# Attention with prompt tokens on one core: a context loaded earlier, its transposes three steps ahead, and first-stage work put in another order

## The chip, the cores and the metric

The kernel runs on one core of one Trainium2 chip. The metric is the device time in microseconds (us) of one execution. The engines are named as the profile names them: PE is TensorE's matmul stream (PEld its weight loads), DVE is VectorE, ACT is ScalarE, POOL is GpSimd, SP is SyncE. SP computes nothing here; it issues DMAs, in program order, and so does ACT's own queue (ACTq) in between ACT's instructions.

## The reference

Cross-attention over eight sequences. `x` is 8 x 112 x 320, the context 8 x 375 x 512, of which the last 4 tokens are image-prompt tokens and the first 371 are text. There are 20 heads of 16 channels. All is 32-bit floating point.

```python
q   = heads(x @ W_q)                               # 20 heads x 16
k_t = heads(text @ W_k);   v_t = heads(text @ W_v)
probs_t  = softmax(q @ k_t.T * 16 ** -0.5)
text_out = probs_t @ v_t
k_ip = heads(ip @ W_k_ip); v_ip = heads(ip @ W_v_ip)
qsem = l2norm(probs_t @ text)                      # per head
fused = q @ k_ip.T * 16 ** -0.5 + 0.5 * (qsem @ l2norm(ip).T)
ip_out = (softmax(fused) * mask) @ v_ip
out = (text_out + ip_out) @ W_out + b_out + x
```

## The kernel before

**Sequences and steps.** The eight sequences are numbered b = 0 to 7. The 20 heads are taken in five groups of four, so that there are 40 steps (b, g) with g = 0 to 4. The four heads of a group stand on the four 32-partition strips of TensorE.

**What a step does.** `multiplied` (L734) multiplies the transposed, unnormalised probabilities of the group, tile `xgT`, with the tile `u`, which holds the Gram matrix of the context, prompt columns and the group's values next to each other. Between its blocks TensorE computes the scores of the group two steps ahead (`scores`, L679), VectorE their negated maxima (`probabilities`, L692), ScalarE the exponentials (L696), and SP writes these probabilities into a ring of two tiles `xg` (L705). VectorE turns the next step's `xg` into `xgT` (`transposed`, L715), reduces the products in PSUM (`reduced`, L782), and GpSimd puts the next group's values into `u` (`placed`, L648). A function `between` then does a piece of the work for the next sequence on each step: the Gram matrix (L495), values (L571), keys (L537, or L528 for the last third of the heads), and queries (L332, L340).

**Where a sequence's data comes from.** `load_ctx` loads a context into a tile `ct`. Contexts 0 and 1 are loaded at the start and transposed on TensorE in three chunks (L410), each copied from PSUM into `ctxT` (L418 on VectorE, L420 on ScalarE). From context 2 on the load is laid out so that VectorE can do the transposing, in three instructions (L400), one in each of three steps. Such a load is eight DMAs on SP (L140, L145) and a small memset on GpSimd (L138). The Gram matrix is evacuated to the tile `ug` and from there written into `u` with four DMAs for each of four blocks (`gram_to_groups`, L513). Values go from `vext` to DRAM (`vd`, L587) and come back laid out for the groups (`vr`, four DMAs, L596).

**First stages.** Before step (0, 0) a fixed sequence of calls prepares sequence 0, and as much of sequence 1 as step (0, 0) needs: Gram matrix, values, queries (in six pieces), keys (in three), the scores and probabilities of steps (0, 0) and (0, 1), the transposes of context 1, and the first third of the values of sequence 1. On TensorE, SP and VectorE the order of the program is the order of execution everywhere; on ScalarE and GpSimd it is so in the first stages, and on ScalarE in the steps too. GpSimd's order in the steps is chosen by the scheduler.

**PSUM banks.** There are eight: four of a pool `ps_qd`, two of `ps_sc` for scores, and two of `ps_mm` for the rest. `bank(name)` takes one of `ps_mm`, or with `spare=True` one of `ps_sc`. In the first stages half of the early scores take banks of `ps_qd` as well. Context 1's transposes take banks of `ps_mm`.

**Where the loads of the steps stand.** `load_rest(n)` runs once in each step, after the reductions: step 0 loads two sequences of x, step 1 context 2 (`load_next(2)`), step 2 the output weights, step 3 the mask and the bias.

Of the kernel before, what the change touches and what calls it, by code (L numbers as in the profile page):

```python
# [20 lines left out]
def kernel(  # L21
# [63 lines left out]
    def bank(name, spare=False):  # L85

        if spare:
            return ps_sc.tile([P, 512], F32, tag="sc", name=name)
        return ps_mm.tile([P, 512], F32, tag="mm", name=name)
# [28 lines left out]
    def load_embed(eng, t, w):  # L118
        eng.dma_start(t[:, :, :C], w.rearrange("(p e) f -> p e f", e=NE))

    def spread(eng, t):

        v = t[:, :, FULL * P :].rearrange("p k (a r d) -> p k a r d", r=2, d=D)
        for a in (3, 2, 1):
            eng.tensor_copy(v[:, :, a, 0, :], v[:, :, a // 2, a % 2, :])
        eng.memset(v[:, :, :, 1, :], 0.0)
# [188 lines left out]
    def project_queries(bs):  # L315
        n = len(bs)
        xT = work.tile([P, NC, 2 * S], F32, tag="xT", name=f"xT_{bs[0]}", bufs=1)
        qm = work.tile([P, NC, 2, 2 * S], F32, tag="qm", name=f"qm_{bs[0]}", bufs=2)

        qT = const.tile([P, NC, S], F32, tag="qT", name="qT") if bs[0] == 0 else None  # L320
        for j, b in enumerate(bs):
            queries[b] = (qT, qm, j)
        nc.gpsimd.memset(xT[REST:, FULL, :], 0.0)
        for i in range(NC):
            cn = min(P, C - i * P)
            if bs[0] == 0:

                ps = ps_qd.tile([P, 512], F32, tag="qd", name=f"ps_x_0_{i}")
            else:
                ps = bank(f"ps_x_{bs[0]}_{i}", spare=bs[0] > 1 and i > 0)  # L330
            for j, b in enumerate(bs):
                nc.tensor.transpose(  # L332
                    ps[:cn, j * S : (j + 1) * S], x_sb[:, b, i * P : i * P + cn], ident[:S, :S]
                )
            nc.scalar.copy(xT[:cn, i, : n * S], ps[:cn, : n * S])
            yield
        for i in range(NC):
            ps = bank(f"ps_q_{bs[0]}_{i}")
            for j in range(NC):
                nc.tensor.matmul(  # L340
                    ps[:, : n * S],
                    wq_sb[:, j, i * P : (i + 1) * P],
                    xT[:, j, : n * S],
                    start=(j == 0),
                    stop=(j == NC - 1),
                )

            for r in range(2 if i < FULL else 1):
                nc.vector.tensor_scalar_mul(  # L349
                    qm[:, i, r, : n * S], ps[:, : n * S], emask[:, r : r + 1]  # L350
                )
            if qT is not None:
                nc.scalar.copy(qT[:, i, :], ps[:, :S])
            yield
# [37 lines left out]
    def transposed_context(b):  # L392
        begin(b)
        s = st[b]
        ct, ctxT = s["ct"], s["ctxT"]
        if b >= LEAD:

            for c in range(NT):
                some = slice(c * QN, (c + 1) * QN)
                nc.vector.transpose(  # L400
                    ctxT[:, :, c * P : (c + 1) * P].rearrange("p e (j i) -> p j e i", i=RG),
                    ct[:, some, :].rearrange("p j (k e) -> p j e k", e=NE),
                )
                yield
            return
        for c in range(NT):
            rows = min(P, TT - c * P)
            ps = bank(f"ps_c_{b}_{c}")
            for e in range(NE):
                nc.tensor.transpose(  # L410
                    ps[:, e * P : e * P + rows],
                    chunk(ct[:, c, :], e)[:rows],
                    ident[:rows, :rows],
                )
            o = ctxT[:, :, c * P : c * P + rows]
            i = ps.rearrange("p (e t) -> p e t", t=P)[:, :, :rows]
            if c % 2 and b < 1:
                nc.vector.tensor_copy(o, i)  # L418
            else:
                nc.scalar.copy(o, i)  # L420
            yield
# [84 lines left out]
            doubled(ps[c][:, : T - c * P], c, half[:, c])  # L506
            yield

    def gram_to_groups(b, blocks):

        for q in blocks:
            for a in range(GROUP):
                nc.sync.dma_start(  # L513
                    st[b]["u"][a * RG : (a + 1) * RG, q * GW : (q + 1) * GW],
                    ug[q * RG : (q + 1) * RG, :],
                )
# [69 lines left out]
    def values_to_dram(b, eng, c0=0, c1=NT):  # L586
        eng.dma_start(  # L587
            st[b]["vd"][c0 * P : c1 * P].rearrange("(c p) x -> p c x", p=P),
            st[b]["vext"][:, c0:c1, :C],
        )  # L590
# [460 lines left out]
    def drain(*gens):  # L1051
        for gen in gens:
            for _ in gen:
                pass
# [5 lines left out]
    def run(key, make, pieces=1):  # L1060

        if key not in gens:
            gens[key] = make()
        for _ in range(pieces):
            next(gens[key], None)

    def between(b, g):

        nb = b + 1
        new = nb < B  # L1070


        first = [bs for bs in pairs if bs[0] == (nb if b == 0 else nb + 1)]
        rest = [bs for bs in pairs if bs[0] == nb]
        if g == 0:
            if new:
                run(("g", nb), lambda: gram(nb), 2)
            if new:
                run(("g", nb), None)
            if b == 0:  # L1080
                run(("v", nb), None)
            if b > 0 and new:
                run(("f", b - 1), lambda: finish(b - 1))
        if g == 1:
            if new:
                run(("v", nb), lambda: values(nb), 1 if b == 0 else 2)
            if b == 0:
                run(("pp",), prompt_projections)
            for bs in first if b == 0 else ():
                run(("q", bs[0]), lambda: project_queries(bs), 3)  # L1090
        if g == 2 and new:
            run(("v", nb), None)
            run(("k", nb), lambda: keys(nb))
            for bs in first if b == 0 else ():
                run(("q", bs[0]), None)
        if g == 2 and b > 0 and new:
            run(("f", b - 1), None, 2)
        if g == 3:
            if new:
                run(("k", nb), None, 1)  # L1100
            if b > 0 and new:
                run(("f", b - 1), None)
            for bs in first if b > 0 else ():
                run(("q", bs[0]), lambda: project_queries(bs), 3)
            if b == 0:
                run(("t", b), lambda: prompt_logits(b))
            for bs in rest:
                run(("q", bs[0]), None)
        if 0 <= g - 2 * (b == 0) < NT and nb + 1 < B:
            run(("c", nb + 1), lambda: transposed_context(nb + 1))  # L1110
        if g == 4:
            if b > 0 and new:
                run(("f", b - 1), None, 2)
            if nb < B - 1:
                run(("k", nb), None, 1)
            for bs in (first if b > 0 else []) + rest:
                run(("q", bs[0]), None)
# [12 lines left out]
    order_values()  # L1130
    drain(products)
    nc.scalar.preload_act_table(AF.Exp)
    gram_to_groups(0, range(QN))
    run(("v", 0), lambda: values(0))
    run(("q", 0), lambda: project_queries(pairs[0]), 3)
    run(("v", 0), None, 2)
    values_to_dram(0, nc.scalar)
    spread(nc.gpsimd, wq_sb)
    nc.gpsimd.tensor_copy(wv_sb[:, :, C:], wk_sb[:, :, FULL * P : C])
    spread(nc.gpsimd, wk_sb)  # L1140
# [3 lines left out]
    for a in range(GROUP):  # L1144
        scores(0, 0, a, early=True)
        probabilities(0, 0, a)
    run(("q", 0), None)
    values_to_groups(0)
    for a in range(GROUP):
        if a == 2:  # L1150
            run(("k", 0), None)
        scores(0, 1, a, early=True)
        probabilities(0, 1, a)
    load_embed(nc.sync, wkip_sb, w_k_ip)
    load_embed(nc.sync, wvip_sb, w_v_ip)
    transposed(0, 0)
    placed(0, 0)
    drain(transposed_context(1))
    run(("k", 0), None)
    run(("v", 1), lambda: values(1))  # L1160
    more_constants()
# [5 lines left out]
    def load_rest(n):  # L1167

        if n == 0:
            load_x(1, 3)  # L1170
        elif n == 1:
            load_next(2)
        elif n == 2:
            load_channels(nc.sync, wo_sb, w_out)
        elif n == 3:
            nc.sync.dma_start(sm_sb, smask.unsqueeze(1))
            nc.sync.dma_start(bias_sb, b_out.partition_broadcast(S))
        elif n == NG:
            load_x(3, 5)
        elif n == 2 * NG:  # L1180
            load_x(5, B)
# [198 lines left out]
```

## Time and profile before

| | us |
|---|---|
| median of three timed runs | 436.21 |
| the three runs | 433.45, 436.21, 437.04 |
| the profiled execution, its own time | 437.43 |
| its span | 435.7 |
| mean granted clock of TensorE | 0.992 |
| first stages end, step (0, 0) begins | 40.36 |
| steps (0, 1) to (0, 4) begin | 52.76, 64.94, 74.30, 86.46 |
| step (1, 0) begins | 96.36 |

A step's beginning is the start of its first L734 on PE in the timeline. A line of the timeline has the start, the duration, the engine, the line of the kernel, the operation, what it writes and reads, the shape and the count; in brackets stands how long the engine was idle before it and what ended that idle time. Neighbouring instructions of one kind are merged into one line. SPq and ACTq are DMA issues on the queues of SP and ACT. A line of the list of waits has the waiting engine, tile and line, what it waited for, and the total in us, the number of waits and the longest one. A line of the table by stretches has the stretch, its length, and then for PE, PEld, DVE, ACT and POOL the busy time and the number of instructions, then the granted clock (1.00 is full speed), the busy share of the DMA engines and GB/s.

### The profile page before, as it was taken

To read this page: it belongs to the slowest core of one execution; us is meant where nothing else is said; L and a number is where in the kernel's file an instruction comes from. 1 tells how busy PE (TensorE), PEld (TensorE's weight loads), DVE (VectorE), ACT (ScalarE), POOL (GpSimd) and SP (SyncE) were. 2 spreads that over 40 slices of the span, in tenths; PEclk is the share of its full clock that TensorE was granted. 3 is DMA by queue.
4 is the path that set the end of the run, shared out by engine and by line. 5 is a ranking of instruction groups with operands and counts; after the bars stand their busy time and mean duration, and the time that the engine had idled before them with its cause. 6 is when DMAs were issued, how large, how long until landed. Compare 5 with 4: busy or idle time off the path is not lost. (4 is left out here: it accounts for less than half of the span.)

```text
span 435.7 us, 13984 instructions
## 1 busy us (share of the span) xinstructions
PE 420.6 (97%) x5521; PEld 328.1 (75%) x5521; DVE 325.9 (75%) x669; ACT 190.9 (44%) x663; POOL 111.9 (26%) x276
## 2 busy tenths in 40 slices
PE   8999999889999999999999999999999999999986
PEld 7856767668777887788777887788777887776783
DVE  5044468688797988888797988988787877878874
ACT  2352342223534363333535363433534353436793
POOL 6301100011133121602124111602124111526440
PEclk9998999989999999999999999999999999999999
DMA  7577357678556766458556766459565636553300
GB/s 253 150 186 214 90 129 170 162 174 192 130 156 144 180 171 164 128 141 205 138 147 147 171 139 168 123 134 205 133 168 133 160 89 179 150 146 106 95 4 26
DMA packets 57630, 64.26 MB, mean 147 GB/s; under 512 B 18448, under 2 KB 51592, under 8 KB 57566
## 3 DMA queue, kind: packets, MB, share of 16 engines
q1 hardware_dynamic: 57000, 62.66, 56.7%
q8 instruction: 43, 0.70, 0.7%
q10 hardware_dynamic: 566, 0.72, 0.5%
q14 instruction: 21, 0.17, 0.1%
HBM read 18.67 MB, written 5.32 MB: 55 GB/s over the span
## 5 line engine op out<-in xcount | busy, mean ns | idle before, releaser
L734 PE MATMUL ps_qd<-u,xgT 32*112 32x328 f32 (+11 forms) x3840 | 219.3, 353 | 0.6 <-POOL shared L769 0.6
L734 PEld LDWEIGHTS ps_qd<-u,xgT 32*112 32x112 f32 x3840 | 186.5, 172 | 34.4 <-issue 11.9
L715 DVE STREAM_TRANSPOSE xgT<-xg 128x1536 f32<-128x1536 f32 (+1 forms) x45 | 119.1, 2668 | 10.6 <-DMA xg<-p 9.8
L696 ACT ACTIVATE p<-ps_s,nmx 112x371 f32<-112x371 f32 x160 | 87.0, 581 | 85.9 <-DVE nmx L692 64.1
L692 DVE TENSOR_REDUCE nmx<-ps_s 112x1 f32<-112x371 f32 x160 | 77.6, 528 | 53.6 <-PE ps_s L679 52.4
L782 DVE CUSTOM_DVE_ANT_0 junk<-ps_qd,p 112x371 f32<-112x371 f32 x148 | 80.3, 543 | 15.5 <-ACT vext L578 0.5
L679 PE MATMUL ps_s<-kT,qm 32*112 32x375 f32 (+1 forms) x320 | 66.3, 484 | 0.7 <-ACT shared L765 0.7
L648 POOL COPY u<-vr 128x64 f32<-128x64 f32 x120 | 26.0, 237 | 154.1 <-PE ps_qd L734 104.8
L571 PE MATMUL ps_v<-wv_sb,ctxT 128*128 128x384 f32 (+1 forms) x192 | 63.6, 480 | 0.0
L571 PEld LDWEIGHTS ps_v<-wv_sb,ctxT 128*128 128x128 f32 x192 | 35.2, 190 | 19.7
L537 PE MATMUL ps_k<-ctxT,wk_sb 128*128 128x371 f32 x136 | 47.6, 494 | 0.0
L747 ACT COPY pvs<-ps_qd 112x21 f32<-112x21 f32 x150 | 15.7, 189 | 62.0 <-PE ps_qd L734 62.0
L537 PEld LDWEIGHTS ps_k<-ctxT,wk_sb 128*128 128x128 f32 x136 | 25.7, 196 | 15.5 <-issue 1.1
L679 PEld LDWEIGHTS ps_s<-kT,qm 32*112 32x112 f32 x320 | 26.8, 172 | 6.2 <-ACT kT L544 2.1
L495 PE MATMUL ps_g<-ctxT 128*32 128x375 f32 (+11 forms) x672 | 30.4, 333 | 0.0
L495 PEld LDWEIGHTS ps_g<-ctxT 128*32 128x32 f32 x672 | 27.7, 110 | 2.0
L698 ACT COPY ipl<-ps_s 112x4 f32<-112x4 f32 x140 | 23.5, 168 | 0.0
L578 ACT COPY vext<-ps_v 128x384 f32<-128x384 f32 (+1 forms) x24 | 11.2, 467 | 24.3 <-PE ps_v L571 24.3
L349 DVE TENSOR_SCALAR qm<-ps_q,emask 128x224 f32<-128x224 f32 (+1 forms) x25 | 9.1, 397 | 16.3 <-PE ps_q L340 16.2
L400 DVE STREAM_TRANSPOSE ctxT<-ct 128x512 f32<-128x512 f32 x18 | 19.9, 1104 | 0.0
L340 PE MATMUL ps_q<-xT,wq_sb 128*128 128x224 f32 (+1 forms) x90 | 17.8, 335 | 2.1 <-ACT kT L544 2.1
L544 ACT COPY kT<-ps_k 128x371 f32<-128x371 f32 x17 | 8.0, 470 | 24.7 <-PE ps_k L537 24.6
(167 smaller groups left out, 321.9 us busy)
## 6 DMA issues: line engine op xcount, KB each, us to landing
xg<-p SPq DMA_DIRECT2D x159, 162.3 KB
u<-ug SPq DMA_DIRECT2D x128, 99.0 KB
ct<-in_ctx_dram SPq DMA_DIRECT2D x24, 176.0 KB
vr<-vd SPq DMA_DIRECT2D x32, 120.0 KB
vip<-vipd SPq DMA_DIRECT2D x6, 560.0 KB
vd<-vext SPq DMA_DIRECT2D x7, 320.0 KB
vd<-vext SPq DMA_DIRECT2D x7, 160.0 KB
out_dram<-ob SPq DMA_DIRECT2D x8, 140.0 KB
```

The lines of the kernel that those rows point to most:

```text
L400: nc.vector.transpose(ctxT[:, :, c * P : (c + 1) * P].rearrange("p e (j i) -> p j e i", i=RG), ct[:, some, :].rearrange("p j (k e) -> p j ...
L495: nc.tensor.matmul(ps[c][q * RG : (q + 1) * RG, j * RG - c * P : T - c * P], ctxT[:, e, j * RG : (j + 1) * RG], ctxT[:, e, j * RG : T], st ...
L537: nc.tensor.matmul(ps[:, :TT], wk_sb[:, e, i * P : (i + 1) * P], s["ctxT"][:, e, :TT], start=(e == 0), stop=(e == NE - 1),)
L571: nc.tensor.matmul(ps[:, :w], ctxT[:, e, c * P : (c + 1) * P], wv_sb[:, e, :w], start=(e == 0), stop=(e == NE - 1),)
L648: nc.gpsimd.tensor_copy(v, dealt(b, c, s["vr"][:, c * QN : (c + 1) * QN, g, :]))
L679: nc.tensor.matmul(ps[:S, :w], qm[a * RG : (a + 1) * RG, i, r, j * S : (j + 1) * S], s["kT"][a * RG : (a + 1) * RG, i, :w], start=True, st ...
L692: nc.vector.tensor_reduce(nmx, ps[:S, :TT], AX.X, ALU.max, negate=True)
L696: nc.scalar.activation(p, ps[:S, :TT], AF.Exp, bias=nmx)
L698: nc.scalar.copy(s["ipl"][:, groups[g][a], :], ps[:S, TT:T])
L715: nc.vector.transpose(xT[:, j : j + n].rearrange("p j (k q) -> p q j k", q=QN), xg[:, :, j * RG : (j + n) * RG].rearrange("p q (j k) -> p ...
L734: nc.tensor.matmul(banks[a][:S, j * RG : UW], xT[a * RG : (a + 1) * RG, j, :S], region(b, c)[a * RG : (a + 1) * RG, q, j * RG - c * P :], ...
L782: nc.vector.tensor_tensor_reduce(out=junk, in0=ps[:S, :TT], in1=s["p", g][:, a, :], scale=1.0, scalar=0.0, op0=ALU.mult, op1=ALU.add, accu ...
```

## The change

Six things are edited, all in what is done for sequences 0, 1 and 2:

- Context 1's transposes run right after the first four scores, ahead of the last queries and the second keys. Their first two chunks take banks of `ps_qd`, the third one of `ps_mm`, and the third chunk is copied by VectorE (before, all three of context 1 were copied by ScalarE). For context 0 nothing changes in this.
- Context 2 is loaded at the end of the first stages instead of in step 1, and its three transposes run in steps 0, 1, 2 of sequence 0 instead of in steps 2, 3, 4.
- The second piece of the keys of sequence 0 runs ahead of all four scores of step (0, 1), not between the second and the third.
- The last of the four blocks of `gram_to_groups(0)` is issued on ScalarE's queue, after the first three pieces of the queries.
- `values_to_groups(0)` is issued on SP right after the write to `vd`, ahead of the writes of the first probabilities.
- The transposes of queries 1 and 2 take banks of `ps_sc` for their second and third part, as those of later queries did before. `placed(0, 0)` now stands ahead of `transposed(0, 0)`; they are on different engines.

```diff
@@ project_queries
-                ps = bank(f"ps_x_{bs[0]}_{i}", spare=bs[0] > 1 and i > 0)
+                ps = bank(f"ps_x_{bs[0]}_{i}", spare=i > 0)
@@ transposed_context
-            ps = bank(f"ps_c_{b}_{c}")
+            if b > 0 and c < 2:
+                ps = ps_qd.tile([P, 512], F32, tag="qd", name=f"ps_c_{b}_{c}")
+            else:
+                ps = bank(f"ps_c_{b}_{c}")
...
-            if c % 2 and b < 1:
+            if c == 1 + b:
                 nc.vector.tensor_copy(o, i)
             else:
                 nc.scalar.copy(o, i)
@@ gram_to_groups
-    def gram_to_groups(b, blocks):
+    def gram_to_groups(b, blocks, eng=nc.sync):
...
-                nc.sync.dma_start(
+                eng.dma_start(
@@ between
-        if 0 <= g - 2 * (b == 0) < NT and nb + 1 < B:
+        if g < NT and nb + 1 < B:
             run(("c", nb + 1), lambda: transposed_context(nb + 1))
@@ first stages
-    gram_to_groups(0, range(QN))
+    gram_to_groups(0, range(QN - 1))
     run(("v", 0), lambda: values(0))
     run(("q", 0), lambda: project_queries(pairs[0]), 3)
+    gram_to_groups(0, (QN - 1,), nc.scalar)
     run(("v", 0), None, 2)
     values_to_dram(0, nc.scalar)
+    values_to_groups(0)
...
     for a in range(GROUP):
         scores(0, 0, a, early=True)
         probabilities(0, 0, a)
+    drain(transposed_context(1))
     run(("q", 0), None)
-    values_to_groups(0)
+    run(("k", 0), None)
     for a in range(GROUP):
-        if a == 2:
-            run(("k", 0), None)
         scores(0, 1, a, early=True)
         probabilities(0, 1, a)
     load_embed(nc.sync, wkip_sb, w_k_ip)
     load_embed(nc.sync, wvip_sb, w_v_ip)
+    placed(0, 0)
     transposed(0, 0)
-    placed(0, 0)
-    drain(transposed_context(1))
+    load_next(2)
     run(("k", 0), None)
     run(("v", 1), lambda: values(1))
@@ load_rest
-        elif n == 1:
-            load_next(2)
```

## The prediction

> **What bounds the kernel now.** I read the page first, for the engine that is never short of work.
>
> ```profile
> span 435.7 us, 13984 instructions
> PE 420.6 (97%) x5521; PEld 328.1 (75%) x5521; DVE 325.9 (75%) x669; ACT 190.9 (44%) x663; POOL 111.9 (26%) x276
> ```
>
> TensorE is busy for 420.6 of 435.7 us. A change that leaves its matmuls alone, as this one does, can only save the rest: 15.1 us of idle time, and whatever is lost to a lower clock. So the second view was TensorE's own list of waits, from 28 to 110 us, where the edited lines run:
>
> ```profile
> PE ps_q L340 <- ACT kT L544: 2.1, 1, 2.1
> PE ps_k L528 <- ACT ipl L698: 1.9, 1, 1.9
> PE ps_c L410 <- ACT ctxT L420: 1.1, 1, 1.1
> PE ps_x L332 <- ACT ipkv L290: 0.7, 1, 0.7
> ```
>
> Four waits, 5.8 us, all beside edited lines. The third view was the table by stretches of half a microsecond, whose last columns are granted clock, DMA share and GB/s:
>
> ```profile
> 33.00:33.50 0.50, 0.50 (x3) 0.50 (x4) 0.28 (x1) 0.42 (x1) 0.00 (x0) 0.64 1.13 215
> ...
> 36.50:37.00 0.50, 0.50 (x3) 0.32 (x2) 0.00 (x0) 0.00 (x0) 0.44 (x2) 0.95 0.79 202
> ...
> 83.50:84.00 0.50, 0.00 (x0) 0.00 (x0) 0.50 (x3) 0.44 (x1) 0.00 (x0) 1.00 0.53 178
> ...
> 94.50:95.00 0.50, 0.50 (x3) 0.47 (x2) 0.36 (x3) 0.44 (x1) 0.05 (x1) 0.58 0.72 172
> ...
> 97.50:98.00 0.50, 0.50 (x8) 0.19 (x4) 0.02 (x1) 0.00 (x0) 0.16 (x2) 0.51 1.18 294
> ```
>
> The clock is granted at one half between these pairs of rows. A mean of 0.64 in the first means that the drop came at 33.14, a mean of 0.95 in the second that it ended at 36.55; the later stretch runs in the same way from 94.58 to 97.99. Each lasts 3.4 us at half speed, so each costs 1.7 us of matmul time. They follow the wait at 32 us and the one at 92 us; the wait at 83 us has no such tail.
>
> **The first stages.** The fourth view was the timeline. TensorE from the first scores to step 0 (start, duration):
>
> ```profile
> 24.70 0.89 PE L679 MATMUL ps_s<-kT,qm 32*112 32x371 f32 x8
> 25.52 0.92 PE L340 MATMUL ps_q<-xT,wq_sb 128*128 128x112 f32 x6
> ...
> 27.18 2.76 PE L537 MATMUL ps_k<-ctxT,wk_sb 128*128 128x371 f32 x8
> 30.68 1.23 PE L410 MATMUL ps_c<-ident,ct 128*128 128x128 f32 x8
> 32.99 1.04 PE L410 MATMUL ps_c<-ident,ct 115*128 115x115 f32 x4 [1.08 <-ACT ctxT L420]
> 33.22 2.94 DVE L715 STREAM_TRANSPOSE xgT<-xg 128x1536 f32<-128x1536 f32 x1 [1.37 <-DMA xg<-p]
> 33.83 4.02 PE L537 MATMUL ps_k<-ctxT,wk_sb 128*128 128x371 f32 x8
> 37.69 2.74 PE L571 MATMUL ps_v<-wv_sb,ctxT 128*128 128x384 f32 x8
> 40.36 1.22 PE L734 MATMUL ps_qd<-u,xgT 32*112 32x392 f32 x10
> ```
>
> The third transpose of context 1 waited 1.08 us for a bank, and the keys after it took 4.02 us where the same eight matmuls had taken 2.76. After the change the order is: scores of step 0, all twelve transposes, last queries, second keys, scores of step 1 together, third keys, values. At full clock these cost, from start to start, 0.82 (24.70 to 25.52), 1.85 (12/8 of 1.23), 0.85, 2.69, 0.82, 2.69 and 2.67 (37.69 to 40.36): 12.4 us. The 0.85 and 2.69 are 0.92 and 2.76 less 0.07, by which the 2.74 of the values runs into what follows. Step 0 could start at 37.1 instead of 40.36, 3.2 us sooner: 1.7 of it the clock, 1.1 the bank, 0.4 the scores of step 1, which now run in one block.
>
> VectorE now copies the third chunk out of its bank, and the second keys use that bank next. Such a copy was made once for context 0:
>
> ```profile
> 7.54 0.67 DVE L418 COPY ctxT<-ps_c 128x512 f32<-128x512 f32 x1
> ```
>
> It queues behind the maxima of step 0, about where the 0.85 us of queries run on TensorE. I take nothing, with its own 0.7 us as the upper bound; ScalarE is spared it.
>
> Now the queues that were reordered.
>
> ```profile
> 14.90 11.69 SPq L513 DMA_DIRECT2D u<-ug  x16
> 18.72 0.42 ACT L578 COPY vext<-ps_v 128x320 f32<-128x320 f32 x1 [1.59 <-PE ps_v L571]
> 20.68 0.82 PE L340 MATMUL ps_q<-xT,wq_sb 128*128 128x112 f32 x6
> 21.33 0.42 ACTq L587 DMA_DIRECT2D vd<-vext  x1
> 26.78 3.69 SPq L705 DMA_DIRECT2D xg<-p  x4
> 30.53 2.09 SPq L596 DMA_DIRECT2D vr<-vd  x4
> 43.19 1.74 SPq L705 DMA_DIRECT2D xg<-p  x2
> ```
>
> Four of the sixteen u writes go to ScalarE's queue. On SP one costs 0.73 us (11.69/16), on ScalarE the one issue shown costs 0.42. They fall into the 1.59 us that ScalarE idles before the copy at 18.72, and delay it by 0.1 to 1.3 us. That copy frees the bank of the queries at 20.68, so up to about 1.5 us is covered: cost nothing, at worst 0.5 if the issues slow one another down. SP is done with u at 23.7 instead of 26.6.
>
> The added wait is worse placed. The four vr reads now stand on SP ahead of the first xg writes, and they wait until vd, issued on ScalarE at 21.33, has landed. The DMA view of 24 to 25 us shows the last packets of ScalarE's queue:
>
> ```profile
> q10 hardware_dynamic: 10, 0.00, 1.3%
> ```
>
> So vd's data ends soon after 24, and with its completion lands at 24.5 to 26. Queued behind vr are the four xg writes of step 0, those of step 1, two prompt weights and the load of context 2. With vd landed at 25, vr is issued to 27.1 and the xg writes to 30.8, where they now end at 30.5. The transpose that starts at 33.22 then starts at 33.5 and ends at 36.5, in time for 37.1. At 26, or if vr's packets hold up xg's on the engines for their 2.09 us, it ends up to 2 us later and step 0 starts 1.5 us late. I take 0.3 us; below nothing it can't go, as TensorE is then the later one. First stages: 3.2 less 0.3 is 2.9 us.
>
> **The load of context 2, the eight DMAs.** They leave step 1 and go ahead of the write at 43.19, into a stretch in which SP has nothing else; there they cost nothing, since what is behind them (the xg of step 2) is transposed a whole step later. What they leave:
>
> ```profile
> 62.81 2.27 SPq L140 DMA_DIRECT2D ct<-in_ctx_dram  x4
> ...
> 66.48 4.19 SPq L513 DMA_DIRECT2D u<-ug  x4
> 67.11 1.03 ACT L696 ACTIVATE p<-ps_s,nmx 112x371 f32<-112x371 f32 x2 [1.72 <-DVE nmx L692]
> ...
> 73.33 2.48 SPq L513 DMA_DIRECT2D u<-ug  x4
> 75.92 1.83 SPq L705 DMA_DIRECT2D xg<-p  x2
> 80.25 2.95 DVE L715 STREAM_TRANSPOSE xgT<-xg 128x1536 f32<-128x1536 f32 x1 [3.15 <-DMA xg<-p]
> 85.13 1.40 PE L340 MATMUL ps_q<-xT,wq_sb 128*128 128x224 f32 x6 [2.13 <-ACT kT L544]
> ```
>
> The probabilities computed from 67.11 on can be written out only after 70.67, because SP is in the context load from 62.81 to 66.48 and then in u writes slowed by it (4.19 us against 2.48 for the next four). The other half goes out at 75.92, VectorE's transpose waits 3.15 us for it, the maxima and exponentials behind it slip, ScalarE's key copy with them, and TensorE stands for 2.13 us. Taking 3.7 us of issues and 1.7 us of slowing off SP puts every one of these writes over 3.15 us earlier, so VectorE doesn't wait. What is late next is the key copy itself, which follows its matmuls with the prompt logits in between: near nothing. Gain 2.1 us.
>
> **The three transposes of context 2** move from steps 2, 3, 4 to 0, 1, 2. Step 2 keeps one. In the other two they follow the reductions, where VectorE then idles:
>
> ```profile
> 54.35 0.99 DVE L692 TENSOR_REDUCE nmx<-ps_s 112x1 f32<-112x371 f32 x2 [5.13 <-PE ps_s L679]
> 66.53 0.99 DVE L692 TENSOR_REDUCE nmx<-ps_s 112x1 f32<-112x371 f32 x2 [4.96 <-PE ps_s L679]
> 87.30 1.09 DVE L400 STREAM_TRANSPOSE ctxT<-ct 128x512 f32<-128x512 f32 x1
> 93.89 0.54 PE L528 MATMUL ps_k<-ident,k 128*128 128x128 f32 x3 [1.88 <-ACT ipl L698]
> ```
>
> 1.09 us into gaps of 5.13 and 4.96 is free; without the cover, if context 2 landed more than 4 us into the gap, each would delay the maxima behind it. At 87.30 the transpose stands ahead of the maxima, the next big transpose and the maxima that the wait at 93.89 hangs on. Taking it out shortens that wait by 1.1 us, leaving 0.8. The half-speed stretch at 94.58 began after this wait; with 0.8 us of idling instead of 1.88 I take it as gone, 1.7 us. The transpose in step 4 stood beside reductions: nothing.
>
> **The query banks.** The 0.7 us wait of L332 goes, since two of its three banks now come from the scores' pair. But the next scores then wait for the copies out of these banks, so I take 0.3 of 0.7 (bounds 0 and 0.7).
>
> **The sum**, against the profiled execution's 437.43 us: 2.9 + 2.1 + 1.1 + 1.7 + 0.3 = 8.1, so 429.3 us. The three timed runs before spread from 433.45 to 437.04 around 436.21; two half-speed stretches are 3.4 us, so such stretches coming and going may be all of that spread, and the profiled run has both.
>
> **Rivals.** First, the half-speed stretches are not the waits' doing. For it: 2.13 us of idling at 83 us left the clock at 1.00. Against: both begin within 0.7 us of the end of a wait. Then 3.4 of the 8.1 us stay: 432.7 us. [...] The rows at 33 and 94 us speak against it, the row at 83 us for it. Chance 0.13.
>
> Second, SP stays late in steps 2 and 3 without the load, as the u writes alone keep it busy, so that the 2.13 us wait and what follows remain. Then only the first stages and 0.3 are won: 434.2 us. The 2.48 us of an undisturbed group speaks against it. Chance 0.09.
>
> Third, slower: the vr wait on SP. If vd lands late, xg, the transpose of step 0 and all later steps go with it, one for one from a landing at about 25.6 us. At 33.7 it has eaten the 8.1 us, and from 36.9 on the kernel is over 1% slower: 440.6 us. For it: vd now shares its queue. Against: its packets end soon after 24. Chance 0.08.
>
> **The numbers.** My forecast has 0.70: its own range is 427.5 to 431.5 (all of the 0.8 and 0.3 won too, or 1.5 us lost to vr and 0.5 to ScalarE's queue). To hold the first rival and half of the second the range goes from 427.0 to 433.5. A change of 1%, about what a measurement of this kernel can tell, is 431.85 against the median. Faster by over 1%: 0.70 and the lucky end of the first rival, 0.71. Within 1%: 0.21, the first two rivals. Slower: 0.08.
>
> **What would show it.** In the changed kernel: step 0's first L734 at 37 to 38 us; no wait of L410 on L420; eight context DMAs on SP before step 0; the clock at 1.00 from 30 to 40 and from 80 to 100; L715 in step 3 with no wait for xg; L340 with no 2 us wait in step 3; L528's first wait below 1 us. The forecast is wrong if vr's wait on SP moves step 0 beyond 40 us, if context 2 isn't there when VectorE comes to it in step 0, or if half-speed stretches appear elsewhere.

## The result and the profile after

The changed kernel's median is 432.05 us (15 runs, 430.63 to 435.12), against 435.32 us before (15 runs, 433.45 to 438.43): the ratio is 0.9913, with a 95% interval of 0.9886 to 0.9939. That is 3.3 us by the medians, a gain, but below the 1% line. The forecast of 429.3 us was 2.8 us too low. The time lies outside the forecast's own range, 427.5 to 431.5, and inside the one that was widened to hold two rivals, 427.0 to 433.5. Of its chances, 0.71 stood on a gain over 1% and 0.21 on less; it was less.

The profiled execution took 432.11 us, with a span of 430.1 us, 5.6 us less than the span of the profile before; TensorE's idle time in it fell from 15.1 to 11.3 us. The page, and TensorE's list of waits over the whole span (the tile and line that waited, for what, us in total, times, longest):

```profile
span 430.1 us, 13979 instructions
...
PE 418.8 (97%) x5521; PEld 327.3 (76%) x5521; DVE 326.8 (76%) x670; ACT 190.1 (44%) x662; POOL 111.6 (26%) x276
```

```profile
PE ps_w L430 <- POOL ident masks.py:199: 1.5, 1, 1.5
PE ps_qd L737 <- DVE xgT L718: 1.3, 1, 1.3
PE ps_k L531 <- ACT ipl L701: 1.1, 1, 1.1
PE ps_a L891 <- ACT bT L972: 1.0, 1, 1.0
...
PE ps_k L540 <- DVE ctxT L421: 0.2, 1, 0.2
```

Three of the four waits shown before are gone. The key transposes in step 4 (now L531) still wait, 1.1 us. L430 waits at the very start, as it did before; L737 and L891 lie in the last 20 us. Lines of the kernel after the edit to the context transposes are three higher than before.

The timeline of the first stages in the changed kernel:

```profile
25.00 0.89 PE L682 MATMUL ps_s<-kT,qm 32*112 32x371 f32 x8
...
25.17 1.88 SPq L599 DMA_DIRECT2D vr<-vd  x4
...
25.82 1.70 PE L413 MATMUL ps_c<-ident,ct 128*128 128x128 f32 x12
...
27.14 9.53 SPq L708 DMA_DIRECT2D xg<-p  x8
...
28.40 2.76 PE L540 MATMUL ps_k<-ctxT,wk_sb 128*128 128x371 f32 x8 [0.21 <-DVE ctxT L421]
...
33.81 2.97 DVE L718 STREAM_TRANSPOSE xgT<-xg 128x1536 f32<-128x1536 f32 x1
...
37.19 1.22 PE L737 MATMUL ps_qd<-u,xgT 32*112 32x392 f32 x10
```

Twelve transposes run in one piece of 1.70 us, the second keys wait 0.21 us for VectorE's copy, the transposition of the probabilities starts without waiting for the DMA, and step 0 begins at 37.19 us: 12.19 us after the first scores, where the sum had 12.39. SP's vr issue at 25.17 shows vd's landing, which the sum had at 25.

Later in the changed kernel:

```profile
73.35 2.95 DVE L718 STREAM_TRANSPOSE xgT<-xg 128x1536 f32<-128x1536 f32 x1
...
79.38 1.40 PE L340 MATMUL ps_q<-xT,wq_sb 128*128 128x224 f32 x6
...
82.30 0.99 DVE L695 TENSOR_REDUCE nmx<-ps_s 112x1 f32<-112x371 f32 x2 [0.67 <-PE ps_s L682]
...
87.22 0.54 PE L531 MATMUL ps_k<-ident,k 128*128 128x128 f32 x3 [1.08 <-ACT ipl L701]
...
89.57 0.17 PEld L737 LDWEIGHTS ps_qd<-u,xgT 32*112 32x112 f32 x1 [0.43 <-DVE ss L785]
```

The first two rows carry no bracket: in step 3 neither VectorE nor TensorE waits any more. The last row is new. At the start of step (1, 0) TensorE waits for VectorE's reductions of step (0, 4) (L785), which free the PSUM banks.

The starts of the steps, from the first L734 (L737) of each on TensorE, for the profiled execution of every kernel of this study but the last (e10), whose edit lies behind them. The labels are those of the experiments; the column of (0, 4) and (1, 0) is their sum.

| us | step 0 begins | (0,1) + (0,2) | (0,3) | (0,4) + (1,0) | (1,1) begins |
|---|---|---|---|---|---|
| before, first profile | 40.36 | 21.54 | 12.16 | 20.32 | 106.78 |
| before, second profile (e5) | 39.12 | 21.53 | 11.96 | 18.70 | 103.72 |
| changed | 37.19 | 21.04 | 10.08 | 18.48 | 99.19 |
| e1, before with fillers | 38.81 | 21.53 | 12.46 | 19.37 | 104.57 |
| e2, first stages only | 36.85 | 21.03 | 11.60 | 18.69 | 100.58 |
| e3, load only | 38.80 | 21.53 | 10.09 | 18.50 | 101.33 |
| e4, load early, turned late | 37.29 | 21.04 | 10.08 | 18.68 | 99.49 |
| e6, query bank back | 37.38 | 21.54 | 10.09 | 18.47 | 99.88 |
| e7, SP order back | 36.90 | 21.04 | 10.10 | 18.46 | 98.90 |
| e8, two sums off VectorE | 37.16 | 21.04 | 10.09 | 17.76 | 98.45 |
| e9, e8 with fillers near the end | 37.38 | 21.04 | 10.08 | 17.77 | 98.68 |

The first scores start anywhere from 24.66 to 25.20 us, so the first column has 0.5 us of its own scatter. From there to step 0 it is 12.18 or 12.19 us in every kernel with the new first stages, and 14.10 or 14.11 in e1, e3 and e5. Step 0 itself takes 12.40 or 12.41 us in all of them.

### The profile page after: what moved, and what is told of

Same layout as the page of the kernel before. It is cut to its first block, busy times and chain, and to the rows that moved or that the text cites. A ratio compares the mean times of both kernels' runs of the same rounds, so it can differ in the third digit from the quotient of the medians.

```text
span 430.1 us, 13979 instructions
## 1 busy us (share of the span) xinstructions
PE 418.8 (97%) x5521; PEld 327.3 (76%) x5521; DVE 326.8 (76%) x670; ACT 190.1 (44%) x662; POOL 111.6 (26%) x276
## 5 line engine op out<-in xcount | busy, mean ns | idle before, releaser
L737 PE MATMUL ps_qd<-u,xgT 32*112 32x328 f32 (+11 forms) x3840 | 220.1, 353 | 1.3 <-DVE xgT L718 1.3
L737 PEld LDWEIGHTS ps_qd<-u,xgT 32*112 32x112 f32 x3840 | 187.0, 172 | 34.5 <-issue 10.9
L718 DVE STREAM_TRANSPOSE xgT<-xg 128x1536 f32<-128x1536 f32 (+1 forms) x45 | 119.1, 2667 | 11.4 <-DMA xg<-p 10.8
L785 DVE CUSTOM_DVE_ANT_0 junk<-ps_qd,p 112x371 f32<-112x371 f32 x148 | 80.2, 542 | 15.5 <-ACT kT L536 0.5
L540 PE MATMUL ps_k<-ctxT,wk_sb 128*128 128x371 f32 x136 | 46.3, 483 | 0.2 <-DVE ctxT L421 0.2
L400 DVE STREAM_TRANSPOSE ctxT<-ct 128x512 f32<-128x512 f32 x18 | 20.0, 1109 | 1.9 <-DMA ct<-in_ctx_dram 1.9
L581 ACT COPY vext<-ps_v 128x384 f32<-128x384 f32 (+1 forms) x24 | 11.3, 471 | 21.2 <-PE ps_v L574 21.2
L471 POOL TENSOR_TENSOR ug<-ug,half 128x128 f32<-128x128 f32 (+1 forms) x24 | 10.4, 446 | 32.0 <-ACT ug L470 32.0
L928 POOL TENSOR_TENSOR wv<-vip,w 112x1280 f32<-112x1280 f32 x6 | 14.8, 2465 | 14.2 <-DVE w L868 14.2
```

The lines of the kernel that those rows point to most:

```text
L400: nc.vector.transpose(ctxT[:, :, c * P : (c + 1) * P].rearrange("p e (j i) -> p j e i", i=RG), ct[:, some, :].rearrange("p j (k e) -> p j ...
L540: nc.tensor.matmul(ps[:, :TT], wk_sb[:, e, i * P : (i + 1) * P], s["ctxT"][:, e, :TT], start=(e == 0), stop=(e == NE - 1),)
L718: nc.vector.transpose(xT[:, j : j + n].rearrange("p j (k q) -> p q j k", q=QN), xg[:, :, j * RG : (j + n) * RG].rearrange("p q (j k) -> p ...
L737: nc.tensor.matmul(banks[a][:S, j * RG : UW], xT[a * RG : (a + 1) * RG, j, :S], region(b, c)[a * RG : (a + 1) * RG, q, j * RG - c * P :], ...
L785: nc.vector.tensor_tensor_reduce(out=junk, in0=ps[:S, :TT], in1=s["p", g][:, a, :], scale=1.0, scalar=0.0, op0=ALU.mult, op1=ALU.add, accu ...
```

## The experiments

**e1: the clock.** The kernel before, with matmuls of no use in two of its waits.

```diff
@@ transposed_context, ahead of the third chunk of context 1
+            if (b, c) == (1, NT - 1):
+                fill = ps_qd.tile([P, 512], F32, tag="qd", name="ps_fill_0")
+                for _ in range(4):
+                    nc.tensor.matmul(fill[:, :P], ident, ident, start=True, stop=True)
@@ keys, ahead of the last third of sequence 1
+            if (b, i) == (1, FULL):
+                fill = bank("ps_fill_1")
+                for _ in range(7):
+                    nc.tensor.matmul(fill[:, :P], ident, ident, start=True, stop=True)
```

> The kernel before, with matmuls of no use put into two of its waits: four of 128 columns ahead of the third transpose of context 1 (wait of 1.08 us) and seven ahead of the key transposes in step 4 (wait of 1.88 us). They write banks that nobody reads. Theory 'the waits bring the half-speed stretches': with the waits filled the clock stays at 1.00 from 30 to 40 us and from 90 to 100 us, the third keys take 2.8 us instead of 4.0, and the mean clock of the runs is 0.999 or so; the median falls by what such stretches cost in the typical run of before, 0.5 to 2 us (434.8 to 433.3). [...]

The median was 434.62 us against 434.86 (ratio 0.9983, 0.9956 to 1.0011): no difference. Three of its 12 runs had a mean clock below 0.998, against 10 of the 35 runs of before beside it, so the fillers did not make half speed clearly rarer, and 12 runs are few to tell; none of the 12 went as low as 0.992, as 5 of the 35 did. In the profile the clock stayed up at 32 and 92 us, and step 0 began at 38.81, but a half-speed stretch came after the wait that had been left unfilled, at 83 us, where the first profile of before had none. The theory did not come out as written: in the profiles the stretches follow waits, but not the same waits in each execution.

**e2: the first stages alone.** The changed kernel without the load and the turning of context 2.

```diff
-        if g < NT and nb + 1 < B:
+        if 0 <= g - 2 * (b == 0) < NT and nb + 1 < B:
...
-    load_next(2)
...
+        elif n == 1:
+            load_next(2)
```

> The changed kernel with the load of context 2 put back into step 1 and its three transposes into steps 2, 3, 4: only the first stages and the query banks are changed. Theory 'the parts add, each at its place': step 0 begins at 37.2 as in the changed kernel, step 1 takes 11.2, but steps 3 and 4 take 12.2 and 9.5 to 9.9 again; step (1, 1) begins 3.5 to 4 us earlier than before's 106.78, and the median is 1.5 to 2.5 us under before (433.0 to 433.8). Rival 'what is won early is taken back later, whatever it was': the end is as early as in the whole change, 432, with steps of sequences 1 to 6 shorter than the changed kernel's.

Median 433.26 us, ratio 0.9964 (0.9934 to 0.9993), within the forecast of the additive theory. Step 0 begins as in the changed kernel; step 3 keeps its wait (11.60 us). Not as expected: steps (0, 4) and (1, 0) take 18.69 us, almost what they take in the changed kernel, though the transposes of context 2 stand in step 4 again. Step (1, 1) begins 6.2 us earlier than in the first profile of before, more than any theory had, but 3.1 us earlier than in the second (e5).

**e3: the load alone.** The kernel before with the opposite edits: `load_next(2)` behind `placed(0, 0)`, and the transposes in steps 0, 1, 2.

> The kernel before with only this changed: context 2 is loaded at the end of the first stages and turned in steps 0, 1, 2. Theory 'the parts add': step 0 begins at 40.4 as before, steps 3 and 4 take 10.1 and 8.1 to 8.5 instead of 12.2 and 9.9, no half speed after 92 us; step (1, 1) begins 3.5 to 4.5 us earlier than before's 106.78; the median is 1.5 to 2.5 us under before. Rival 'taken back later': 432 as for the whole change. If SP's long stop at the last DMA of the load costs something here, steps 0 and 1 are longer than 12.4 and 12.2.

Median 432.85 us, ratio 0.9945 (0.9925 to 0.9965). Step 3 falls to 10.09 us, and step (1, 1) begins 2.4 us earlier than in e5. By the ratios e2 wins 0.36% and e3 0.55%, together 0.91%, against 0.87% for the whole: within the intervals the parts add. The rival that either part ends as early as the whole falls for e3: at a mean clock of 0.998 or more its median is 432.65 us (11 runs), against 431.08 of the changed kernel (13 runs). For e2 it isn't excluded, with 431.88 in six such runs. Against the 434.69 of before beside them (25 runs) these are gains of 2.0 and 2.8 us, more together than the 3.6 of the whole, so part of the gain may be taken back later. In this execution step 0 began at 38.80 us with the wait of 1.1 us for the transpose bank in place: no half speed followed it.

**e4: load early, turn late.** The changed kernel with the old condition in `between` alone.

> The changed kernel with the load early, but the three transposes of context 2 back in steps 2, 3, 4. Theory 'it was the SP queue in step 3 and VectorE in step 4': step 3 takes 10.1 to 10.3, as in the changed kernel, since SP is free; step 4 and its wait for the prompt logits of the next scores grow by about 1.1 us (L531 waits 1.9 to 2.2 instead of 1.1); the median is 0.5 to 1.5 us over the changed kernel. Rival 'VectorE's transposes caused the wait in step 3 as well': step 3 takes 11 us or more.

Step 3 took 10.08 us, so SP's queue was its cause, as the theory said. But step 4's wait (L531) was 1.2 us, not 1.9 to 2.2, and the pair of steps 18.68 against 18.48. At a mean clock of 0.998 or more the median is 431.09 us (6 runs), the changed kernel's 431.08 (13 runs). At that clock, moving the three transposes is worth nothing that can be measured; the load is what counts. The median over all runs, 432.82 us (0.9930, 0.9902 to 0.9958), lies within the theory's 0.5 to 1.5 us over the changed kernel, but because 6 of its 12 runs had a mean clock below 0.998, against 2 of 15 of the changed kernel. Whether the later transposes bring half speed more often was not settled.

**e5: before, once more.**

> The kernel before, unchanged, for one more profiled execution. Theory 'the half-speed stretches come and go, and the sum of the prediction took two of them for granted': 25 of 35 timed runs of before had a mean clock of 0.998 or more, so most likely this one has none or one; without any, step 0 begins at 38.8 (not 40.4), the wait at 92 us costs about 1.2, steps (0, 4) and (1, 0) together take 18.6 (not 20.3), and step (1, 1) begins at 103.5 to 104.5 (not 106.8). Rival 'the stretches belong to the waits': both are there again and the table is that of the first profile.

This execution took 439.4 us with a mean clock of 0.992, and both stretches lay elsewhere. TensorE's waits from 20 to 110 us:

```profile
PE ps_q L340 <- ACT kT L544: 1.9, 1, 1.9
PE ps_k L528 <- ACT ipl L698: 1.2, 1, 1.2
PE ps_c L410 <- ACT ctxT L420: 1.1, 1, 1.1
PE ps_x L332 <- ACT ipkv L290: 0.7, 1, 0.7
...
```

The table by stretches of the same execution (the column before the last two is the clock):

```profile
422.50:423.00 0.50, 0.00 (x0) 0.00 (x0) 0.50 (x2) 0.50 (x7) 0.00 (x0) 1.00 0.00 0
...
423.50:424.00 0.50, 0.50 (x6) 0.50 (x6) 0.39 (x3) 0.50 (x1) 0.00 (x0) 0.84 0.00 0
...
430.50:431.00 0.50, 0.50 (x6) 0.50 (x5) 0.00 (x0) 0.00 (x0) 0.00 (x0) 0.83 0.00 0
```

All four waits of the prediction are there, and the clock stayed at 1.00 behind each. Instead it fell at 423.8 and came back at 430.7, twice 3.4 us; a wait of 1.0 us near the end had ended 0.7 us before the fall, and one of 1.3 us 8.3 us before it. The wait at 92 us was 1.88 in the first profile and is 1.2 here. The theory's times hold: the pair of steps takes 18.70 us, and step (1, 1) begins at 103.72. This is the undisturbed account of before up to step (1, 1): 103.72 us, of which the change wins 4.5, not 7.6.

**e6: the query bank.** The changed kernel with `spare=bs[0] > 1 and i > 0` again.

> The changed kernel with the transposes of queries 1 and 2 back in banks of ps_mm. Forecast of the term 0.3 us, the step table said 0.5 (steps 1 and 2 together 21.54 before, 21.04 after): steps 1 and 2 take 12.2 and 9.35 again, 21.5 together, and step 3 begins 0.5 us later. Rival 'the bank only moves the wait to the scores': 21.0 to 21.1 together.

Steps 1 and 2 took 21.54 us together, as before, and 21.04 with the edit: 0.5 us, the theory's figure.

**e7: the order on SP and ScalarE's queue.**

```diff
-    gram_to_groups(0, range(QN - 1))
+    gram_to_groups(0, range(QN))
...
-    gram_to_groups(0, (QN - 1,), nc.scalar)
...
-    values_to_groups(0)
...
     run(("q", 0), None)
+    values_to_groups(0)
     run(("k", 0), None)
```

> The changed kernel with the queue order of before in the first stages: all sixteen u writes on SP, and the vr reads after the first four writes of probabilities. Theory 'the order of these DMAs neither cost nor won': step 0 begins at 37.2 to 37.6, and the median is that of the changed kernel within 0.5 us. Rival 'vr was what held step 0, so moving it ahead was needed': GpSimd puts the values of step 0 in place at 36 to 38.5 and step 0 begins at 38 us or later, 0.8 us or more lost.

Step 0 began at 36.90 us, earlier than either theory had, but its first scores were earlier too: 12.19 us lie between them, as in the changed kernel. The median was 431.63 us (0.9928, 0.9893 to 0.9963). The timeline shows how near it was:

```profile
35.69 0.59 POOL L651 COPY u<-vr 128x64 f32<-128x64 f32 x3 [7.35 <-DMA vr<-vd]
...
36.90 0.60 PEld L737 LDWEIGHTS ps_qd<-u,xgT 32*112 32x112 f32 x10 [0.55 <-POOL k L215]
```

With vr behind the probabilities the values are in place at 36.3 us, 0.6 us before TensorE wants them. The two edits to these queues neither cost nor won anything that shows.

**e8: VectorE in step 4.** The changed kernel with the helper `shared` for two of the four reductions of step (0, 4).

```diff
-        if n == len(steps) - NG - 1:
+        if n == len(steps) - NG - 1 or n == NG - 1:
             sums = shared(b, g, GROUP // 2)
             next(sums)
             reduced(b, g, 2)
...
+        if n == NG - 1:
+            next(sums)
+        if n == NG:
+            drain(sums)
```

> The changed kernel with two of the four reductions of step (0, 4) taken from VectorE: ScalarE copies the two products out of PSUM, GpSimd multiplies, ScalarE sums. Theory 'steps (0, 4) and (1, 0) are held by VectorE's row of maxima, turn, maxima and four reductions, which frees the PSUM banks of the next step': (1, 0) falls from 10.35 to 9.9 or less, the pair from 18.5 to 18.0. Rival 'the pair is held by TensorE and the wait for the scores of (1, 1)': the pair stays at 18.4 or more. The median moves by less than can be told, 0.5 us at most.

Step (1, 0) fell from 10.35 to 9.63 us, the pair from 18.48 to 17.76:

```profile
87.54 0.87 ACT L768 COPY shared<-ps_qd 112x371 f32<-112x371 f32 x2
...
88.82 1.22 PE L737 MATMUL ps_qd<-u,xgT 32*112 32x392 f32 x10
```

These are rows of its timeline. ScalarE has emptied two banks by 88.4 us, and the ten matmuls at 88.82 run through. The bound of the pair was VectorE's row of work. The median, 431.52 us of 5 runs (0.9918, 0.9889 to 0.9947), can't show so little.

**e9: the same with fillers near the end.**

```diff
@@ multiplied, ahead of the first block
+        if (b, g) == (B - 1, NG - 1):
+            for _ in range(5):
+                nc.tensor.matmul(banks[0][:, :P], ident, ident, start=True, stop=True)
@@ finish
-                warm(ps, 3)
+                warm(ps, 6)
```

> The kernel of the run with two sums off VectorE, with matmuls of no use in two waits of the last steps: five in the bank of the last step's first product, ahead of it, and three more ahead of the last but one sequence's output sums (six instead of three). They overwrite nothing that is kept. In two of the profiled executions a half-speed stretch began just after these waits of 1.0 to 1.3 us. Theory 'short waits near the end bring half speed in some executions': of its runs at most 1 in 10 has a mean clock below 0.998 (13 of 49 runs of before, 11 of 43 of the kernels with the whole change or nearly so), and the median is 430.6 to 431.3, under the changed kernel's 432.05. Rival 'the fillers change nothing': a quarter of the runs below 0.998 as before, median 431.3 to 432.

Median 430.91 us of 6 runs (429.51 to 431.74), ratio 0.9889 (0.9850 to 0.9929), and none of the 6 below 0.998, while 5 of the 11 runs of before beside it were: as the theory had it. It is the fastest kernel of the study by its median. That it beats the changed kernel is not shown: the intervals overlap, and of e8's 5 runs, without the fillers, none had half speed either.

**e10: one long wait.**

```diff
+        if n == 3 * NG + 3:
+            late = const.tile([P, P], F32, tag="late", name="late")
+            nc.sync.dma_start(late, ehs[0, :P, :P])
+            fill = bank("ps_late")
+            nc.tensor.matmul(fill[:, :P], late, ident, start=True, stop=True)
```

> The changed kernel with one long wait of TensorE in step (3, 3): a matmul of no use that reads a tile whose load SP issues only in that step, behind the step's probabilities; 3 to 6 us of waiting. Theory 'half speed comes by chance after a wait, the likelier the longer it is': the mean clock lies below 0.998 in nearly all of its runs, with a stretch of 3.4 us or more behind this wait, and the time is the changed kernel's plus the wait plus 1.7 us, 436 to 440 in all. Rival 'the stretches have nothing to do with waits': about a quarter of the runs have one, and the time is 435 to 438.

All four runs had a mean clock of 0.990 to 0.992. The median was 439.46 us (1.0103, 1.0047 to 1.0160), 7.4 us over the changed kernel. Clock and time are those that the theory named, and the rival falls ("the likelier the longer" stands on this one length, 6.0 us, beside the waits of 0.9 to 1.9 us of other executions). The list of waits has the new one, and the table by stretches the clock behind it:

```profile
PE ps_late L1222 <- DMA late<-in_ctx_dram: 6.0, 1, 6.0
```

```profile
228.00:229.00 1.00, 0.00 (x0) 0.00 (x0) 0.00 (x0) 0.00 (x0) 0.00 (x0) 0.50 0.64 168
...
233.00:234.00 1.00, 1.00 (x3) 0.43 (x3) 0.00 (x0) 0.00 (x0) 0.55 (x3) 0.50 0.00 0
234.00:235.00 1.00, 1.00 (x4) 0.59 (x3) 0.00 (x0) 0.00 (x0) 0.00 (x0) 0.61 0.00 0
```

In the profile half speed had begun before the wait was over, and lasted into the matmuls behind it until 234.8. The other three runs have no profile; their mean clock is as low. The step took 17.86 us instead of 9.34, 8.5 more: the wait, the added matmul, and the slow matmuls.

## Why the forecast came out as it did

The mechanism held: the load of context 2 leaves a crowded stretch of SP's queue, the first stages lose their bank wait, and nothing that was added costs more than 0.2 us. Two terms of the sum were wrong: 4.3 of its 8.1 us were not there. That the time came within 2.8 us is luck in part: 8.1 us were taken from 437.43, while 3.3 were won from a median of 435.32, and the base that was 2.1 us too slow made up for part of the gain that wasn't there. The time lies in the wide range only because that was stretched to the first rival's 432.7. (The low end of the own range, 427.5, doesn't follow from its terms either: 429.3 less 0.8 and 0.3 is 428.2. Nothing hangs on it.)

**The half-speed stretches (1.7 within the first stages, 1.7 after 92 us; measured: nothing of the median).** This is the step that failed: that the two stretches belong to the two waits in every execution, so that ending the waits would win 3.4 us. In the 60 runs of before beside the experiments the mean clock was 0.998 or more in 42, with a median of 434.6 us, and below in 18, with a median of 437.0. The prediction was made against a profile of the second kind, at 437.43. The second profile of before has the same waits and full speed behind all of them. The changed kernel and two near relatives of it (e4, e7) were below 0.998 in 11 of 37 runs, about as often as before; the changed kernel alone, with 2 of 15, is too few to tell. So it is not shown that the change made half speed rarer: such a stretch also came near the end, 0.7 us after a wait of 1.0 us in e5 and 2.2 us after one of 0.9 us in e4. That these short waits, and not the small matmuls around them, brought it is not shown. At 0.998 or more the medians are 434.6 and 431.1: 3.5 us, where 8.1 less 3.4 and less the 0.9 us of the next term would be 3.8.

**The transposes of context 2 in step 4 (1.1; measured 0.2).** The prediction took the 1.09 us of L400 out of the wait for the key transposes one for one. But without it VectorE only waits for the scores, 0.67 us in the row at 82.30, and the next big transpose starts 0.2 us earlier in the step (2.50 us into it, against 2.71 in e5). The 1.88 us on which the term was built was 1.2 in the other execution of before, so part of it may have belonged to that one. What is then left of the wait hardly matters, since (0, 4) and (1, 0) together are held by VectorE, as e8 showed. The prediction looked for what ends the wait and not for what is late next, one step on.

**The first stages (2.9, of which 1.2 besides the clock; measured 1.9 besides the clock).** From first scores to step 0 it is 14.11 us in e5, 12.19 in the changed kernel. The 0.3 us kept back for vr was not needed. The copy on VectorE cost 0.2.

**Step 3 and the SP queue (2.1; measured 1.9).** Right in size and cause: e2 keeps 11.60 us, e3 and e4 have 10.09 and 10.08, whatever the transposes do.

**The query banks (0.3; measured 0.5).** Right; the scores wait for the copies as was said, 0.69 us, but the two steps together are shorter.

**The load at the end of the first stages (nothing; measured nothing).** It came nearer to a cost than was written, as the timeline of the changed kernel shows:

```profile
37.84 2.27 SPq L140 DMA_DIRECT2D ct<-in_ctx_dram  x4
...
45.70 0.23 SPq L145 DMA_DIRECT2D ct<-in_ctx_dram  x1
...
46.29 3.55 SPq L708 DMA_DIRECT2D xg<-p  x4
...
47.86 1.11 DVE L400 STREAM_TRANSPOSE ctxT<-ct 128x512 f32<-128x512 f32 x1 [1.89 <-DMA ct<-in_ctx_dram]
```

SP stood before the last of the eight DMAs until 45.70, behind transfers of the prompt weights; the trace gives 3.5 us of it to the second of these. The first half of step 2's probabilities, written at 43.19 before, went out at 46.29, and VectorE waited 1.89 us for the context. Both were covered: step 0 took its 12.40 us all the same.

**The rivals.** The first, that the half-speed stretches are not the waits' doing, came nearer: the change did not win the 3.4 us. Its 432.7 us, near the 432.05 measured, is luck in part, since it counts 4.7 us from 437.43. Its mechanism is only half right: e10 ties half speed to a wait of 6.0 us, and in four other profiled executions (both of before, e1 and e4) the stretches come behind waits of 0.9 to 1.9 us, but not always behind the same ones. The second rival, an SP queue that stays late, and the third, vr holding step 0, fell with step 3 and with e7.

**The signs.** In the profile of the changed kernel the clock is 1.00 all through, and step 0, L410, L715 (now L718) and L340 are as the prediction said. Two signs went against it: L528 (now L531) waits 1.08 us and not below 1, and 2 of the 15 timed runs had a mean clock of 0.996 and 0.992, so that half speed does come elsewhere.

**Open.** The change is 4.5 us ahead of e5 at step (1, 1), which is what the measured terms add up to (1.9, 1.9, 0.2 and 0.5), and 3.5 us ahead at the end by the medians at full clock. From step (1, 1) on the executions without half speed there take 329 to 331 us, with steps such as (2, 2) anywhere from 10.6 to 11.8 us whatever was done early. That is wide enough to hide 1 us; whether a part of the gain is given back there was not settled. Nor is it settled what makes one short wait bring half speed and the same wait in another execution not. TensorE's busy time in the 3.41 us just ahead, the length of such a stretch, does not decide it in these traces. In the first profile it was 2.33 us ahead of the fall at 33.14, and 1.53 ahead of the one at 94.58; in e1, by the half-microsecond rows, about 1.75 ahead of the fall at 83.59. In the 3.41 us up to 85.13 in the first profile, with the wait at 83 us in them, it was 1.28 us, and the clock stayed at 1.00.

## What to carry to other kernels

Before a lower clock is put into a sum, look at the clock of many runs: a half-speed stretch behind a wait of a microsecond or two came and went from one execution to the next, and the two profiles of before, each with two such pieces, took 2 and 4 us longer than the median of its runs. When a late transfer is traced to its queue, look at the issues ahead of it on that queue; moving them here to a stretch where nothing behind them is needed soon was worth 1.9 us in step 3, nearly all of the 2.1 that the wait had cost. And follow a shortened wait one step further: the next bound, here VectorE's reductions that free the banks, may stand right behind it (18.48 us for the pair of steps, 17.76 with two reductions off VectorE).

## What the runs showed of the hardware

Half speed came in pieces of about 3.4 us or twice that: 3.41 each in the first profile of before (33.14 to 36.55 and 94.58 to 97.99), 3.4 in e1 (83.59 to 87.01) and e4 (420.93 to 424.34), 6.8 in e5 (423.84 to 430.67) and 6.9 in e10 (227.9 to 234.8). They came behind waits of 0.9 to 1.9 us in the four profiled executions of before, e1, e4 and e5, and in the profile of e10 began within one of 6.0 us; its other three runs have as low a mean clock, 0.990 to 0.992. The eight DMAs of a context load kept SP for 8.1 us behind two weight loads (37.84 to 45.93), of which the trace puts 3.5 us to the landing of the second, against 3.6 us in step 1 of the kernel before.
